# A two-layer graph attention kernel: the order of one superchunk's work within a step

## The chip, the cores and the metric

The kernel runs on one core of one Trainium2 chip. The metric is the device time of one execution in microseconds. The times before are the median of three runs; one more execution was taken with the profiler. In the text PE is TensorE, DVE is VectorE, ACT is ScalarE, POOL is GpSimd and SP is SyncE, the queue that issues most of the plain DMAs.

## The reference

A graph network of two attention layers over 6250 nodes with 256 features, and 200,000 edges that are sorted by destination. For each layer:

```
te  = relu(edge_attr @ We + be) * exp(x @ Wo + bo)[src]
hx  = x @ Wg                                    # 4 heads of 64, then 1 head of 256
al  = leaky_relu((hx . a_s)[src] + (hx . a_d)[dst] + (te @ Wge) . a_e, 0.2)
m   = segment_max(al, dst)
al  = exp(al - m[dst]);  al = al / segment_sum(al, dst)[dst]
out = segment_sum(hx[src] * al, dst) + b
```

Each node has a self loop as well, whose edge term is the mean of its incoming ones. Layer 0 gives relu(out + x), layer 1 adds its input, and residuals of x go on top. A layer norm with a relu stands at the front.

## The kernel before, in words

**Tiles.** The edges of a layer are cut into chunks of 128 and 24 chunks make a superchunk (C = 24); 66 superchunks make a layer. The loop in `edges` goes over the superchunks of both layers, one *step* for each. In a step `st` is the superchunk that is summed, `nx` the one behind it, `pv` the one ahead. The function `ending` writes the last three superchunks of each layer by hand.

**What a superchunk goes through.** `gather` (24 indirect DMAs on POOL, line 1065) brings the source rows of each edge into G; there are three G buffers, so a gather waits until the sums that read its buffer have ended. `spread` (DVE, lines 1189 and 1190) makes one-hot blocks lb and Q from the destinations, for two superchunks at a time. `parts` (line 1304) splits the destinations' logits into three bf16 parts on DVE and multiplies them by Q on PE. `blocks` (DVE, line 1311) lays the result out as aq. `rphase1` (lines 1165 and 1166) makes relu(edge_attr @ We) as y on PE and R on ACT, in two halves; `rphase2` (line 1174) adds its share of the edge logits into the PSUM tile zad, and `adst` (line 1318) the destinations' share, as lb times aq. `edge_rows` (lines 1332 and 1335) transposes zad into rt on DVE, and `logits` (lines 1346 to 1363) makes the logits al and their running maxima fb. `ends` (PE, line 1370) transposes these into the tile lf; `links` (lines 1380 to 1387) runs them over the chunk's rows by two scans on DVE and transposes back; `maxima` (lines 1397 to 1423) takes the maxima and exponentials. `scale` (layer 0, DVE, line 1454) multiplies G by the weights, all 24 chunks in one instruction of 128 x 6144; `scale_rows` (layer 1, ACT, line 1463) does it chunk by chunk. `carried` (lines 1436 to 1444) adds what the superchunk ahead has left for a node that both share. `sums` (PE, line 1473) multiplies the 24 one-hots S, which `onehots` made (DVE, line 1283), by G into u, one matmul of two passes for a chunk. `evict` (ACT, line 1478) copies u to U. `finish` (DVE and ACT, lines 1489 to 1640, transposes at line 1563) does the nodes of `pv`.

**What sets the order.** Each engine takes its instructions in the order in which the code issues them; the framework adds the semaphore waits. So the order of calls in the loop of `edges` is the order on every engine. Before the change a step issues: gather(nx), logits(st), ends(st), spread(nx), parts(nx), the first half of rphase1(nx), links(st), rows2, loads, blocks(nx), maxima(st), the second half of rphase1, rphase2(nx), adst(nx), scale or scale_rows(st), carried(st), sums(st), rows3, onehots(nx), finish(pv), evict(st), edge_rows(nx). The tile lf is one PSUM bank: `ends` writes its columns 1 to 128, and `links` its columns from 160 on.

Of the kernel before, what the change touches and what calls it, by code (L numbers as in the profile page):

```python
# [22 lines left out]
F32 = mybir.dt.float32  # L23
# [8 lines left out]
P = 128  # L32
C = 24
# [48 lines left out]
class Kernel:  # L82
# [705 lines left out]
    def edges(self, ctx):  # L788
        nc = self.nc
        steps = self.steps  # L790
        if self.NS % 2:
            self.load_lb(1)
        pv = late = None
        self.ahead, self.rest = 1, None
        for k, st in enumerate(steps):
            nx = steps[k + 1] if k + 1 < len(steps) else None
            if st["s"] + 2 >= self.NS:
                continue
            for q in steps[k + 1:k + 3]:
                if q["L"] is st["L"] and "tw" not in q:  # L800
                    self.nodes(q)
            self.load_lb(k + 2)
            left = 99
            if self.ahead < len(self.groups):
                left = self.groups[self.ahead][0] - 2 - (self.ahead + 2 >= len(self.groups)) - k
            if self.rest is None and left <= 2:
                gi = self.index_load(self.ahead, self.xp)
                self.rest = self.index_group(self.ahead, self.xp, gi)
            if st["L"].l and (st["s"] == 2 or st["s"] + 3 == self.NS) and not hasattr(self, "flag_i"):
                self.flag()  # L810
                if self.early:
                    self.window()
            if st["s"] + 3 == self.NS:
                self.ending(st, *steps[k + 1:k + 3], pv, late, steps[k + 3] if k + 3 < len(steps) else None)
                pv = late = None
                continue
            if 3 <= k + 1 < 6 and nx["L"].l == 0:
                nx["own"] = steps[k - 2]["G"]
            if k:
                self.gather(nx)  # L820
                st["rows"] = st["L"].l
                drain(self.logits(st))
                self.ends(st)
            self.spread(nx)
            self.parts(nx)
            y = self.rphase1(nx)
            next(y)
            if k:
                self.links(st)
            if late:  # L830
                self.rows2(late)
            self.load_fl(k + 1)
            self.blocks(nx)
            if k:
                drain(self.maxima(st))
            drain(y)
            self.load_ea(k + 2)
            self.rphase2(nx)
            self.adst(nx)
            if "S" not in st:  # L840
                self.onehots(st)
            if k:
                if st["rows"]:
                    self.scale_rows(st)
                else:
                    drain(self.scale(st))
                self.carried(st)
                self.sums(st)
            if late:
                self.rows3(late)  # L850
                late = None
            self.onehots(nx)
            if pv:
                drain(self.finish(pv))
            self.evict(st)
            if pv:
                self.rows1(pv)
                late = pv
            self.index_on(left)
            if k == 4 and self.early:  # L860
                self.lacking()
            if k >= 6:
                next(self.late, None)
                next(self.late, None)
            self.edge_rows(nx)
            if st["s"] + 4 == self.NS:
                drain(self.finish(st))
            pv = st
# [279 lines left out]
    def rphase1(self, st):  # L1148
# [11 lines left out]
        for a, b in self.pieces(c):  # L1160
# [5 lines left out]
            nc.scalar.activation(R[:, :, w], y[:, :, :n], AF.Relu, bias=self.be[l])  # L1166
            yield

    def rphase2(self, st):

        nc, l, R = self.nc, st["L"].l, st["R"]
        for w, o in self.halves(st):
            for i in range(2):
                nc.tensor.matmul(st["zad"][i * PH:(i + 1) * PH, o], self.wea[l][0], R[:, i, w],  # L1174
                                 start=True, stop=False)
# [107 lines left out]
            nc.vector.tensor_tensor(st["S"][:, c0:c1, :], self.k_iota.unsqueeze(1).to_broadcast(w),  # L1283
                                    self.loc[:, o + c0:o + c1].unsqueeze(2).to_broadcast(w), op=OP.is_equal)

    def parts(self, st):

        L, V = st["L"], self.nc.vector
        H = L.H
        if "a3" not in st:  # L1290
            q = [q for q in self.steps[st["k"]:st["k"] + 2 - st["k"] % 2] if q["L"] is L and "tw" in q]
            n, i = len(q), st["k"] % 4
            ad = self.tw4[:, i:i + n, L.ad:L.ad + H]
            a3 = self.wp.tile([P, 2, 4, 3], BF, name="a3")
            r = self.wp.tile([P, 2, 4], F32, name="a3r")
            V.tensor_copy(a3[:, :n, :H, 0], ad)
            V.tensor_sub(r[:, :n, :H], ad, a3[:, :n, :H, 0])
            V.tensor_copy(a3[:, :n, :H, 1], r[:, :n, :H])
            V.tensor_sub(a3[:, :n, :H, 2], r[:, :n, :H], a3[:, :n, :H, 1])
            for j, t in enumerate(q):  # L1300
                t["a3"] = a3[:, j]
        a3 = st["a3"]
        st["zad"] = z = self.ps_1.tile([P, 1024], F32, name="zad")
        self.nc.tensor.matmul(z[:, 400:400 + 3 * H], st["Q"], a3[:, :H, :].rearrange("p h t -> p (h t)"),  # L1304
                              start=True, stop=True)

    def blocks(self, st):

        H = st["L"].H
        st["aq"] = aq = self.aq[st["k"] % 2]  # L1310
        self.nc.vector.tensor_tensor(aq[:, :, 4:4 + 3 * H],
                                     st["zad"][:, 400:400 + 3 * H].unsqueeze(1).to_broadcast([P, 4, 3 * H]),
                                     self.quad.unsqueeze(2).to_broadcast([P, 4, 3 * H]), op=OP.mult)

    def adst(self, st):
# [149 lines left out]
    def sums(self, st, *parts):  # L1465
        nc, L, c = self.nc, st["L"], st["C"]
        G, S = st["G"], st["S"]
        for a, b in parts or ((0, c),):
            for i in range(a, b):
                j = st["n"] = st.get("n", -1) + 1  # L1470
                if j == 0 and "u" not in st:
                    st["u"] = self.ps_1.tile([P, 512], F32, name="u")
                nc.tensor.matmul(st["u"][:, :L.W], S[:, i, :], G[:, i, 0:L.W], start=(j == 0), stop=(j == c - 1))  # L1473
# [282 lines left out]
def drain(g):  # L1756
    for _ in g:
        pass
# [85 lines left out]
```

## Time and profile before

| | before |
|---|---|
| median of 3 runs | 4928.91 us (4916.35 to 4935.57) |
| profiled execution | 4925.46 us |
| its span | 4923.7 us |
| granted TensorE clock | 0.725 of full speed |
| PE busy | 2940.4 us, 60% |
| DVE busy | 2462.7 us, 50% |
| ACT busy | 1132.2 us, 23% |
| POOL busy | 2989.0 us, 61% |
| DMA, mean over the span | 120 GB/s |

The span is the time between the first and the last instruction of the profiled execution. A row of a timeline gives the start, the duration, the engine and line, the operation, the tile written and the tiles read, with shapes, and in brackets how long the engine was idle before and what ended that. "issue" means that the engine waited for nothing that the profile shows, and "remote" a releaser that is not resolved. A row of the waits gives the engine, the tile and line that waited, what it waited for, the microseconds in total, how many times, and the longest. Layer 0's even steps run from about 335 to 2374 us, layer 1's from about 2699 to 4838 us.

### The profile page before, as it was taken

To read this page: it belongs to the slowest core of one execution; us is meant where nothing else is said; L and a number is where in the kernel's file an instruction comes from. 1 tells how busy PE (TensorE), PEld (TensorE's weight loads), DVE (VectorE), ACT (ScalarE), POOL (GpSimd) and SP (SyncE) were. 2 spreads that over 40 slices of the span, in tenths; PEclk is the share of its full clock that TensorE was granted. 3 is DMA by queue.
4 is the path that set the end of the run, shared out by engine and by line. 5 is a ranking of instruction groups with operands and counts; after the bars stand their busy time and mean duration, and the time that the engine had idled before them with its cause. 6 is when DMAs were issued, how large, how long until landed. Compare 5 with 4: busy or idle time off the path is not lost.

```text
span 4923.7 us, 38114 instructions
## 1 busy us (share of the span) xinstructions
PE 2940.4 (60%) x10100; PEld 1841.8 (37%) x10100; DVE 2462.7 (50%) x6148; ACT 1132.2 (23%) x2701; POOL 2989.0 (61%) x3216
## 2 busy tenths in 40 slices
PE   6655666666666666665646556555565555655656
PEld 5433433343333434343434333333333333333334
DVE  5556666676666666666734323333333332333335
ACT  4211111111111111111103323233233332323322
POOL 6356666666666666666544656656666666666663
PEclk8777777777777777777777667667667676666767
DMA  7144444444444444444433434434444443443442
GB/s 223 55 119 125 126 128 134 123 135 132 133 124 128 135 126 131 129 135 122 122 109 92 121 106 115 122 105 119 114 118 114 112 121 107 116 118 107 118 117 71
DMA packets 248253, 591.97 MB, mean 120 GB/s; under 512 B 65849, under 2 KB 105125, under 8 KB 247783
## 3 DMA queue, kind: packets, MB, share of 16 engines
q0 software_dynamic: 150048, 422.51, 32.7%
q1 hardware_dynamic: 97009, 164.82, 10.5%
q10 hardware_dynamic: 976, 2.12, 0.2%
q8 instruction: 86, 1.41, 0.1%
q14 instruction: 134, 1.10, 0.1%
HBM read 544.23 MB, written 45.36 MB: 120 GB/s over the span
## 4 chain that ended last, share of the span: by engine, by line
issue 29%; PE 28%; DVE 21%; POOL 13%; another core or an unknown queue 5%; DMA 3%; ACT 1%; SPq 0%; DVEq 0%; ACTq 0%; POOLq 0%
PE u L1473 21%; POOL G L1065 12%; DVE G L1454 7%; DMA G<-T,src 3%; PE y L1165 2%; DVE S L1283 2%; PE zad L1174 2%; DVE m L1402 1%; DVE lb L1189 1%; DVE rt L1332 1%; ACT R L1166 1%; DVE t1rows L1638 1%; DVE fb L1397 0%; PE lf L1370 0%
## 5 line engine op out<-in xcount | busy, mean ns | idle before, releaser
L1065 POOL DMA_INDIRECT G<-T,src x3066 | 2912.9, 950 | 1824.8 <-issue 949.2
L1473 PE MATMUL u<-G,S 128*128 128x270 f32 (+1 forms) x6212 | 1873.3, 448 | 1419.9 <-issue 1202.2
L1473 PEld LDWEIGHTS u<-G,S 128*128 128x128 f32 x6212 | 1355.8, 221 | 1871.8 <-issue 1438.5
L1463 ACT ACTIVATE G<-G,kw 128x256 f32<-128x256 f32 x1512 | 609.0, 496 | 0.0
L1380 DVE TENSOR_TENSOR_SCAN cl<-fl,cl,lf 4x129 f32<-4x129 f32 (+1 forms) x130 | 61.1, 470 | 1007.6 <-PE zad L1304 940.1
L1478 ACT ACTIVATE U<-u 128x270 f32<-128x270 f32 (+1 forms) x130 | 51.0, 393 | 2169.3 <-PE u L1473 1686.5
L1454 DVE TENSOR_TENSOR G<-G,kps 128x6144 f32<-128x6144 f32 (+6 forms) x86 | 441.7, 5150 | 0.0
L1283 DVE TENSOR_TENSOR S<-kps,loc 128x3072 f32<-128x3072 f32 (+1 forms) x135 | 438.1, 3245 | 4.7
L1165 PE MATMUL y<-ea,webd 64*128 64x256 f32 (+2 forms) x1056 | 355.0, 762 | 41.0 <-ACT R L1166 35.3
L1174 PE MATMUL zad<-R,wea 128*64 128x384 f32 (+1 forms) x1056 | 285.0, 677 | 156.6 <-issue 87.5
L1166 ACT ACTIVATE R<-y,webd 128x1024 f32<-128x1024 f32 (+3 forms) x264 | 235.4, 892 | 427.5 <-PE y L1165 161.9
L1174 PEld LDWEIGHTS zad<-R,wea 128*64 128x64 f32 x1056 | 82.9, 177 | 395.8 <-issue 263.4
L1505 DVE SCALAR_TENSOR_TENSOR mg<-U,mw 128x1 f32<-128x1 f32 x65 | 14.4, 221 | 364.1 <-remote 170.6
L1165 PEld LDWEIGHTS y<-ea,webd 64*128 64x128 f32 x1056 | 116.0, 269 | 105.6 <-issue 59.3
L1332 DVE STREAM_TRANSPOSE rt<-zad 128x768 f32<-128x768 f32 (+1 forms) x130 | 125.8, 968 | 5.4 <-remote 5.4
L567 PE MATMUL fin<-wg,h1T 128*128 128x260 f32 x264 | 116.8, 587 | 1.5 <-ACT h1T L1565 1.5
L1189 DVE TENSOR_TENSOR lb<-lb,kps 128x1536 bf16<-128x1536 bf16 (+1 forms) x68 | 112.9, 1661 | 0.0
L1436 DVE SCALAR_TENSOR_TENSOR G<-U,kw,G 1x257 f32<-1x257 f32 x62 | 29.5, 476 | 152.4 <-issue 87.0
L1575 ACT ACTIVATE t1rows<-t1rows 128x1 f32<-128x1 f32 x66 | 13.4, 203 | 363.9 <-DVE t1rows L571 147.4
L1370 PE MATMUL lf<-ident,fb 128*36 128x128 f32 (+1 forms) x132 | 52.0, 394 | 55.8 <-DVE fb L1363 45.6
L1318 PE MATMUL zad<-lb,aq 128*128 128x384 bf16 (+2 forms) x264 | 83.8, 409 | 0.0
L1515 ACT ACTIVATE mw<-mw 128x8 f32<-128x8 f32 x66 | 13.8, 209 | 298.7 <-issue 146.9
(275 smaller groups left out, 2366.7 us busy)
## 6 DMA issues: line engine op xcount, KB each, us to landing
ea<-in_ea_dram SPq DMA_DIRECT2D x64, 768.0 KB
G<-T,src POOLq DMA_INDIRECT x3066
lb<-locrow SPq DMA_DIRECT2D x64, 384.0 KB
nd<-t1rows SPq DMA_DIRECT2D x66, 225.8 KB
tw<-nd SPq DMA_DIRECT2D x66, 225.8 KB
tw<-T SPq DMA_DIRECT2D x66, 117.2 KB
T<-t1rows SPq DMA_DIRECT2D x66, 113.8 KB
tw<-in_x_dram SPq DMA_DIRECT2D x66, 112.0 KB
```

The lines of the kernel that those rows point to most:

```text
L567: self.nc.tensor.matmul(ps[:, :L.MW], hT[:, k, :], self.wg[L.l][:, k, :], start=(k == 0), stop=(k == 1))
L1065: nc.gpsimd.indirect_dma_start(out=G[:, c, 0:L.TW], out_offset=None, in_=st.get("from", self.T[L.l])[0:self.N, :], in_offset=bass.Indirect ...
L1165: nc.tensor.matmul(y[:, i, :n], self.webd[l][r, :], ea[r, w], start=True, stop=True)
L1166: nc.scalar.activation(R[:, :, w], y[:, :, :n], AF.Relu, bias=self.be[l])
L1174: nc.tensor.matmul(st["zad"][i * PH:(i + 1) * PH, o], self.wea[l][0], R[:, i, w], start=True, stop=False)
L1189: V.tensor_tensor(lb[:, :, :n], lb[:, :, :n], self.k_part.unsqueeze(2).to_broadcast([P, i, n]), op=OP.is_equal)
L1283: nc.vector.tensor_tensor(st["S"][:, c0:c1, :], self.k_iota.unsqueeze(1).to_broadcast(w), self.loc[:, o + c0:o + c1].unsqueeze(2).to_broad ...
L1318: self.nc.tensor.matmul(st["zad"][:, o], st["aq"].rearrange("p k j -> p (k j)"), st["lb"][:, w], start=False, stop=True)
L1332: V.transpose(rv[:, :32 * c].rearrange("p (b n) -> p b n", b=2), z.rearrange("p (b n) -> p b n", b=2)[:, :, :16 * c])
L1454: nc.vector.tensor_tensor(v, v, pw[:, c0:c1, :].unsqueeze(3) .to_broadcast([P, c1 - c0, H, L.F]), op=OP.mult)
L1463: self.nc.scalar.activation(v, v, AF.Copy, scale=st["w"][:, c:c + 1])
L1473: nc.tensor.matmul(st["u"][:, :L.W], S[:, i, :], G[:, i, 0:L.W], start=(j == 0), stop=(j == c - 1))
```

## The change

In a step, links, the first half of rphase1 and maxima now come first. In layer 0 the scaling is cut into two halves of 12 chunks with `carried` between them; `spread` comes behind, then the sums of 14 chunks, `parts` and `blocks`, the sums of 5 chunks, `adst`, and the sums of the last 5. In layer 1 `scale_rows` goes ahead of the second half of rphase1; the sums of 8 chunks come, then `spread` and `parts`, the other 16 chunks, and behind them `rphase2`, `onehots`, `blocks` and `adst`. The product of `parts` lies in columns 240 on of the bank lf, and zad is taken when it is first needed. The first step of all keeps its order.

```diff
-            self.spread(nx)
-            self.parts(nx)
+            else:
+                self.spread(nx)
+                self.parts(nx)
             y = self.rphase1(nx)
             next(y)
             if k:
@@
             self.load_fl(k + 1)
-            self.blocks(nx)
             if k:
                 drain(self.maxima(st))
-            drain(y)
-            self.load_ea(k + 2)
-            self.rphase2(nx)
-            self.adst(nx)
+            else:
+                self.blocks(nx)
+            if k and st["rows"]:
+                self.scale_rows(st)
+                drain(y)
+                self.load_ea(k + 2)
+            else:
+                drain(y)
+                self.load_ea(k + 2)
+                self.rphase2(nx)
             if "S" not in st:
                 self.onehots(st)
-            if k:
-                if st["rows"]:
-                    self.scale_rows(st)
-                else:
-                    drain(self.scale(st))
+            if not k:
+                self.adst(nx)
+                self.onehots(nx)
+            elif st["rows"]:
                 self.carried(st)
-                self.sums(st)
+                self.sums(st, (0, C // 3))
+                self.spread(nx)
+                self.parts(nx, self.lf)
+                self.sums(st, (C // 3, C))
+                self.rphase2(nx)
+                self.onehots(nx)
+                self.blocks(nx)
+                self.adst(nx)
+            else:
+                f = self.scale(st, cuts=(0, C // 2, C))
+                next(f)
+                self.carried(st)
+                drain(f)
+                self.spread(nx)
+                self.sums(st, (0, 14))
+                self.parts(nx, self.lf)
+                self.blocks(nx)
+                self.sums(st, (14, 19))
+                self.adst(nx)
+                self.sums(st, (19, C))
+                if late:
+                    self.rows3(late)
+                    late = None
+                self.onehots(nx)
             if late:
                 self.rows3(late)
                 late = None
-            self.onehots(nx)
...
-    def parts(self, st):
+    def parts(self, st, bank=None):
...
-        st["zad"] = z = self.ps_1.tile([P, 1024], F32, name="zad")
-        self.nc.tensor.matmul(z[:, 400:400 + 3 * H], st["Q"], a3[:, :H, :].rearrange("p h t -> p (h t)"),
+        if bank is None:
+            self.zad(st)
+        st["ad"] = z = st["zad"][:, 400:400 + 3 * H] if bank is None else bank[:, 240:240 + 3 * H]
+        self.nc.tensor.matmul(z, st["Q"], a3[:, :H, :].rearrange("p h t -> p (h t)"),
                               start=True, stop=True)
```

PE in a step of layer 0, before, from the sums of one superchunk to those of the next. The LDWEIGHTS of Q and the matmul of a are `parts`, the matmuls of fin and wg are `finish` and the next layer's node rows, zad from R is `rphase2` and zad from aq is `adst`:

```order
L1473 MATMUL u<-G,S 128x270 x24
L1563 MATMUL fin<-ident,fb 128x128 x2
L1370 MATMUL lf<-ident,fb_195 36x128
L1304 LDWEIGHTS Q
L1304 MATMUL zad<-a_6577,Q 128x12
L1165 MATMUL y<-ea,webd_119 128x256 x2
L1387 MATMUL lf<-ident,cl_189 128x36
L567 MATMUL fin<-wg_894,h1T 128x260 x2
L1165 MATMUL y<-ea,webd_119 128x512 x2
L1174 MATMUL zad<-R,wea_142 64x384 x4
L1318 LDWEIGHTS aq_199
L1318 MATMUL zad<-lb,aq_199 128x384
```

The same engine and layer after the change, from `links` to the last sums:

```order
L1422 MATMUL lf<-ident,cl_190 128x36
L567 MATMUL fin<-wg_894,h1T 128x260 x2
L1192 MATMUL y<-ea,webd_119 128x512 x2
L1207 MATMUL zad<-R,wea_142 64x384 x4
L1508 MATMUL u<-G,S 128x270 x14
L1339 LDWEIGHTS Q
L1339 MATMUL lf<-a_6656,Q 128x12
L1508 MATMUL u<-G,S 128x270 x5
L1353 LDWEIGHTS aq_198
L1353 MATMUL zad<-lb,aq_198 128x384
L1353 LDWEIGHTS aq_198
L1353 MATMUL zad<-lb,aq_198 128x384
```

`parts` and `adst` have moved from ahead of the sums to behind their 14th and their 19th chunk; five chunks follow.

DVE in a step of layer 0, after the change, from the second half of the scaling on; aq from lf is `blocks`, and "waits PE" is a wait for PE's semaphore:

```order
L1489 TENSOR_TENSOR G<-G,kps 128x12x256
L1222 TENSOR_TENSOR lb<-lb,kps 128x1536 [waits DMAHW0_49]
L1223 TENSOR_TENSOR Q<-kps,qsel 128x256
L1329 CAST a_3667<-tw_203 128x8 [waits DMAHW7_49]
L1330 TENSOR_TENSOR a3r<-tw_203,a_3667 128x8 [waits DVE_49]
L1331 CAST a_3667<-a3r 128x8 [waits DVE_49]
L1332 TENSOR_TENSOR a_3667<-a3r,a_3667 128x8 [waits DVE_49]
L1346 TENSOR_TENSOR aq_198<-lf,quad 128x4x12 [waits PE_49]
L571 TENSOR_TENSOR t1rows<-fin,bias_898 128x260 [waits DMAHW5_49,DMAHW4_49]
L1313 COPY kps<-lastloc 128x1
L1316 TENSOR_TENSOR S<-kps,loc 128x3072 [waits DVE_49]
L1524 TENSOR_SCALAR cnt<-U 128x1
```

`blocks` stood between links and maxima and now stands behind the scaling, with rows3, onehots, finish, the transpose rt and the logits queued behind it.

PE in a step of layer 1, after the change:

```order
L1508 MATMUL u<-G,S 128x261 x8
L1339 LDWEIGHTS Q
L1339 MATMUL lf<-a_15150,Q 128x3
L1508 MATMUL u<-G,S 128x261 x16
L1207 MATMUL zad<-R,wea_145 64x384 x4
L1353 LDWEIGHTS aq_199
L1353 MATMUL zad<-lb,aq_199 128x384
L1353 LDWEIGHTS aq_199
L1353 MATMUL zad<-lb,aq_199 128x384
L1405 MATMUL lf<-ident,fb_195 33x128
L1192 MATMUL y<-ea,webd_900 128x256 x2
L1422 MATMUL lf<-ident,cl_190 128x33
```

Here `rphase2` and `adst`, which stood ahead of the sums, follow them, and lf, from which links starts, comes behind.

More of the change, by code (lines that the diff above doesn't have):

```diff
@@ L1167, in rphase1, with zad @@
             yield
+    def zad(self, st):
+        if "zad" not in st:
+            st["zad"] = self.ps_1.tile([P, 1024], F32, name="zad")
     def rphase2(self, st):
+        self.zad(st)
         nc, l, R = self.nc, st["L"].l, st["R"]
@@ L1302, in parts @@
         a3 = st["a3"]
-        st["zad"] = z = self.ps_1.tile([P, 1024], F32, name="zad")
-        self.nc.tensor.matmul(z[:, 400:400 + 3 * H], st["Q"], a3[:, :H, :].rearrange("p h t -> p (h t)"),
+        if bank is None:
+            self.zad(st)
+        st["ad"] = z = st["zad"][:, 400:400 + 3 * H] if bank is None else bank[:, 240:240 + 3 * H]
+        self.nc.tensor.matmul(z, st["Q"], a3[:, :H, :].rearrange("p h t -> p (h t)"),
                               start=True, stop=True)
@@ L1311, in blocks @@
         self.nc.vector.tensor_tensor(aq[:, :, 4:4 + 3 * H],
-                                     st["zad"][:, 400:400 + 3 * H].unsqueeze(1).to_broadcast([P, 4, 3 * H]),
+                                     st["ad"].unsqueeze(1).to_broadcast([P, 4, 3 * H]),
                                      self.quad.unsqueeze(2).to_broadcast([P, 4, 3 * H]), op=OP.mult)
```

## The prediction

> **What bounds the kernel now.** First the page's groups and its chain, then the waits of both layers' steady steps, then the timeline of single steps.
>
> ```profile
> L1065 POOL DMA_INDIRECT G<-T,src x3066 | 2912.9, 950 | 1824.8 <-issue 949.2
> issue 29%; PE 28%; DVE 21%; POOL 13%; another core or an unknown queue 5%; DMA 3%; ACT 1%; SPq 0%; DVEq 0%; ACTq 0%; POOLq 0%
> ```
>
> No engine is busy throughout, and the largest share of the chain is "issue", time without a visible cause. The gathers take 0.95 us each and idle 0.30 us between them ("issue"), so 24 of them take 24 × 1.25 = 30 us per step. The waits of layer 0 (335 to 2374 us, first two rows) and of layer 1 (2699 to 4838 us):
>
> ```profile
> POOL G L1065 <- PE fin L1563: 217.1, 35, 25.0
> POOL G L1065 <- PE u L1473: 138.4, 22, 9.2
> POOL G L1065 <- PE zad L1304: 376.5, 58, 8.3
> ```
>
> Once per step POOL waits for PE, on average 6 us: the G buffer is free when the sums before last have ended. So a step is 30 us of gathers and a wait for the end of the sums. Its length comes from the evictions:
>
> ```profile
> 334.89 0.40 ACT L1478 ACTIVATE U<-u 128x270 f32<-128x270 f32 x1 [3.11 <-PE u L1473]
> 2373.84 0.40 ACT L1478 ACTIVATE U<-u 128x270 f32<-128x270 f32 x1 [12.10 <-PE u L1473]
> 2698.95 0.39 ACT L1478 ACTIVATE U<-u 128x261 f32<-128x261 f32 x1 [20.02 <-PE u L1473]
> 4838.28 0.39 ACT L1478 ACTIVATE U<-u 128x261 f32<-128x261 f32 x1 [21.38 <-PE u L1473]
> ```
>
> Layer 0: 2038.95 us over 58 steps, 35.15 each. Layer 1: 2139.33 over 59, 36.26 each. Why the sums end so late, a layer 0 step shows:
>
> ```profile
> 1018.79 0.94 POOL L1065 DMA_INDIRECT G<-T,src  x1 [4.69 <-PE fin L1563]
> 1022.72 6.54 DVE L1454 TENSOR_TENSOR G<-G,kps 128x6144 f32<-128x6144 f32 x1
> 1026.20 0.50 PE L1318 MATMUL zad<-lb,aq 128*128 128x384 bf16 x2
> 1030.03 0.20 DVE L1444 SCALAR_TENSOR_TENSOR G<-U,slink,G 1x5 f32<-1x5 f32 x1
> 1030.29 13.44 PE L1473 MATMUL u<-G,S 128*128 128x270 f32 x45 [3.60 <-DVE crow L1442]
> 1030.68 3.36 DVE L1283 TENSOR_TENSOR S<-kps,loc 128x3072 f32<-128x3072 f32 x1
> 1041.23 0.97 DVE L1332 STREAM_TRANSPOSE rt<-zad 128x768 f32<-128x768 f32 x1
> 1047.72 0.94 POOL L1065 DMA_INDIRECT G<-T,src  x1 [0.30 <-issue]
> 1049.46 0.61 PE L1473 MATMUL u<-G,S 128*128 128x270 f32 x1 [2.47 <-issue]
> 1053.57 0.94 POOL L1065 DMA_INDIRECT G<-T,src  x1 [4.90 <-PE fin L1563]
> ```
>
> The 45 passes (two per chunk) take 13.44 us, 0.30 each, and then the last ones come one by one with 2.5 us of "issue" between. PE is stuck until some 5 us after the last gather at 1047.72; POOL goes on 34.8 us after its restart. Layer 1 is alike:
>
> ```profile
> 3607.05 0.47 DVE L1380 TENSOR_TENSOR_SCAN cl<-fl,cl,lf 1x129 f32<-1x129 f32 x1 [16.01 <-PE zad L1304]
> 3607.07 0.94 POOL L1065 DMA_INDIRECT G<-T,src  x1 [7.00 <-PE zad L1304]
> 3612.15 9.67 ACT L1463 ACTIVATE G<-G,kw 128x256 f32<-128x256 f32 x24
> 3612.31 2.83 PE L1174 MATMUL zad<-R,wea 128*64 128x384 f32 x8 [1.21 <-issue]
> 3615.07 0.82 PE L1318 MATMUL zad<-lb,aq 128*128 128x384 bf16 x2
> 3615.68 8.60 PE L1473 MATMUL u<-G,S 128*128 128x261 f32 x36
> 3626.49 0.98 DVE L1332 STREAM_TRANSPOSE rt<-zad 128x768 f32<-128x768 f32 x1
> 3628.34 0.59 PE L1473 MATMUL u<-G,S 128*128 128x261 f32 x1 [3.12 <-issue]
> 3641.07 2.77 PE L1473 MATMUL u<-G,S 128*128 128x261 f32 x6 [1.53 <-issue]
> 3644.12 0.94 POOL L1065 DMA_INDIRECT G<-T,src  x1 [7.25 <-PE zad L1304]
> 3649.66 0.60 PE L1473 MATMUL u<-G,S 128*128 128x261 f32 x2
> 3679.13 0.94 POOL L1065 DMA_INDIRECT G<-T,src  x1 [5.21 <-PE zad L1304]
> ```
>
> Here 36 passes run freely, those from 3624 crawl, and at 3641.07, 34.0 us after the restart, PE is free. One more place shows that what crawls is also PE's signals to other engines. POOL gathered without a long pause up to 309:
>
> ```profile
> 290.31 0.27 PE L1370 MATMUL lf<-ident,fb 128*36 128x128 f32 x1
> 308.98 0.40 ACT L1478 ACTIVATE U<-u 128x270 f32<-128x270 f32 x1 [23.47 <-issue]
> 309.22 0.94 POOL L1065 DMA_INDIRECT G<-T,src  x1 [0.59 <-issue]
> 312.52 0.47 DVE L1380 TENSOR_TENSOR_SCAN cl<-fl,cl,lf 4x129 f32<-4x129 f32 x1 [20.45 <-remote]
> 323.64 11.21 PE L1473 MATMUL u<-G,S 128*128 128x270 f32 x48 [1.01 <-DVE G L1444]
> ```
>
> The sums that stand ahead of lf were through at 290.3, but ACT evicted them only at 308.98, and DVE took lf at 312.52, 22 us late. With POOL silent (the wait of 25.0 among the waits, up to 335) all 48 passes of 323.64 run without a pause and the eviction follows at once (334.89). So I read: while gathers run, PE's signals back up, PE itself goes on until something is full (36 passes in layer 1, 17 us after the restart; 45 in layer 0), and what it finished is heard by the others only 34 us after the restart. The backing up must begin before PE is stuck, so before +17.
>
> **The change, part by part.**
>
> *Layer 0, the order on PE.* Before, parts and blocks of the next superchunk stand at the step's start and adst ahead of the sums: all is heard early. After, PE does 14 chunks, the matmul of parts, 5 chunks, adst, 5 chunks; adst waits for blocks on DVE, and blocks for parts on PE. This is a new round trip PE to DVE to PE in the midst of the gathers. Scale in halves lets the sums start 3.3 us sooner (half of 6.54), so +8.2 after POOL's restart instead of +11.5; 28 passes at 0.30 end at +16.6, and parts' signal stands in line behind what they left. I take it that it is heard, and blocks starts, at +34.0. From there the path is: blocks and hand-overs 0.3; adst 0.50 to 0.82; the last 10 passes 3.0 (at 0.30) to 4.6 (at 2.77/6); and what is left of chunks 14 to 19 when PE is stuck, 0 to 2.7 (38 passes are needed; 45 ran freely here, 36 in layer 1; at most I allow six at 0.46, as in 3641.07). The sum is 37.8 to 42.4 us. I take 39.5, near the low end, since the freely running 45 passes are layer 0's own row: 4.35 over 35.15, and 58 × 4.35 = +252 us (ends 58 × 2.65 = +154 and 58 × 7.25 = +420).
>
> Behind blocks on DVE stand onehots, finish, rt and the logits, which now run after +34 instead of under the sums. From onehots (1030.68) to the end of rt (1042.20) is 11.5 us, so lf comes no earlier than 34.2 + 11.5 = 45.7, which is 6.2 in the next gathers. Links to sums were 11.5 and are 8.2: the sums start at 14.4, their 14th chunk ends at 22.8, still ahead of 34.0. So this costs nothing more as long as it stays within those 11 us; the upper end holds the case that it doesn't.
>
> Spread's group on the page, with 68 instructions for 132 superchunks:
>
> ```profile
> L1189 DVE TENSOR_TENSOR lb<-lb,kps 128x1536 bf16<-128x1536 bf16 (+1 forms) x68 | 112.9, 1661 | 0.0
> ```
>
> *Spread, parts' casts, rows3 and carried between the halves* lie on DVE beside the first 14 chunks (8.4 us of PE). Were DVE later than PE there, PE would wait ahead of +34, which costs nothing as long as it waits to +34 anyway; without that wait it is at most spread's 1.66 us in every second step. POOL's and SP's issues keep their order but for the load of ea, a few rows up. Nothing for these.
>
> *Layer 1.* Parts goes behind 8 chunks, but blocks stands behind the sums, so PE doesn't wait in their midst. What costs is that rphase2 and adst, ahead of the sums before, now follow them, and rt, the logits, lf and links wait for them. Behind the sums' end: rphase2 up to 2.83, adst 0.82, rt 0.98, then the logits. Before, rt stood in the shadow of the sums (3626.49) and links began with POOL's restart (3607.05 against 3607.07). So links come 4.6 us later by these rows, and by the logits on top, but rphase2 and adst (3.65) no longer stand between links and sums, and ACT's scaling no longer waits behind the second R. The sums start 0 to 3 us later. Of a later start the two steps shown give the price: started 8.61 after the restart, the step took 37.05; started 5.54 after it, 35.01: 0.66 per us. That is 0 to +2.0 us; I add 0.5 to the upper end for the two instructions of parts that now stand within the sums. I take +1.3, past the middle since the logits' own time isn't in the 4.6: 59 × 1.3 = +77 (0 to +148).
>
> The sum: 4925.46 + 252 + 77 = 5254. The profiled execution lies 3.45 under the median 4928.91 (span 4923.7, the rest about the ends), so 5258 against the median; I say 5255. Ends of this case: 4929 + 154 = 5083 to 4929 + 568 = 5497.
>
> A clock row speaks for a gain in layer 0:
>
> ```profile
> 1030.00:1036.00 6.00, 5.71 (x13) 4.36 (x14) 5.50 (x16) 0.81 (x3) 4.73 (x5) 0.50 0.67 178
> ```
>
> After 3.60 us without a matmul the granted clock is 0.50 and 13 passes take 5.71 us, 0.44 each, against 11.21/48 = 0.23 for the quiet row. If PE idles less before the sums, these 13 cost 2.7 us less. The Trainium skill ("TensorE: Matmul & The Clock Gate", section "Why this matters for your kernels") warns of idle gaps over about 3 us between bursts; the row agrees, and by that rule the halves would spare 2.7 us of each step's sums. Those 2.7 us end before the stuck stretch and are worth something only in the first rival.
>
> **The rivals.**
>
> 1. *The round trip is heard in time (faster).* Parts' matmul at +16.6 is at the edge of the stretch; if DVE hears it at once, PE doesn't wait, and the earlier, warmer sums (3.3 + 2.7 us) all end before +34.0. Then every layer 0 step is POOL's 34.0 and 0.5 for the hand-over: 58 × (34.5 − 35.15) = −38, and layer 1 from 0 to a gain of −0.5 per step if the scaling's earlier start wins, half of that taken (59 × 0.25 = 15): 4929 − 38 − 15 = 4876. It decides if PE's signals at +17 take under 5 us. Against it: 290.31 to 312.52. For it: at the step's start DVE follows PE at once (3607.05 beside 3607.07). The Trainium skill ("Advanced Engine Details and Errata", section "Network/Comms") puts the reading of a semaphore at 50 to 100 ns; by that rule the round trip would be free and this rival the forecast, but the 22 us of the row disagree. Chance 0.15.
> 2. *It cancels.* As 1, but layer 1 pays 0.6: 4929 − 38 + 35 = 4926. Chance 0.05.
> 3. *Late, but not to the end.* PE's signals trickle, blocks hears after 10 us, at +27, and chunks 19 to 24 crawl to +36.5: 58 × 1.35 + 59 × 0.6 = +114, so 5043. Chance 0.14.
>
> **How the numbers follow.** The forecast (blocks waits to +34, layer 1 links late) has 0.66. Range 4900 to 5480: it takes in 2, 3 and the forecast's ends but its last 17 us, and leaves out rival 1 (0.15) and some 0.04 above. The likeliest case's own range is 5083 to 5497. This kernel's measurements tell 0.5% (25 us) from no change. Faster by over that 0.15, within it 0.05, slower 0.14 + 0.66 = 0.80.
>
> **What would show it.** Right: in layer 0, PE idle of over 10 us before adst (L1353), released by DVE aq; DVE idle as long before blocks (L1346); evictions 38 to 42 us apart; in layer 1, rt right behind adst and links 5 us or more after POOL's restart. Wrong: blocks within 2 us of parts' matmul, sums without a wait at chunk 19, layer 0 evictions 34.5 us apart.

## The result and the profile after

| | before | after |
|---|---|---|
| median | 4927.24 us (4 runs, 4916.35 to 4935.57) | 5173.3 us (4 runs, 5165.34 to 5179.9) |
| profiled execution | 4925.46 us | 5174.47 us |
| its span | 4923.7 us | 5172.7 us |
| granted TensorE clock | 0.725 | 0.724 |

The change makes the kernel slower: the ratio is 1.05, 95% interval 1.0474 to 1.0526. The page after, the rows for the gathers, the chain and `blocks` (in group rows: busy time and mean ns, then the engine's idle time ahead of them and what ended most of it):

```profile
PE 23%; DVE 23%; issue 20%; another core or an unknown queue 17%; POOL 12%; DMA 3%; ACT 2%; DVEq 0%; SPq 0%; ACTq 0%; POOLq 0%
L1092 POOL DMA_INDIRECT G<-T,src x3066 | 2916.6, 951 | 2063.0 <-PE u L1508 1014.9
L1346 DVE TENSOR_TENSOR aq<-lf,quad 128x12 bf16<-128x12 f32 (+1 forms) x125 | 24.0, 192 | 1996.1 <-remote 1532.7
```

The gathers take as long as before (0.951 us each), but POOL idles 2063.0 us between them instead of 1824.8, 238 us more. `blocks`, which had no row of its own on the page before, now has DVE idle for 1996.1 us ahead of it. The same four evictions as before (the 4th, 61st, 68th and 127th of the run) in the timeline after:

```profile
340.38 0.38 ACT L1513 ACTIVATE U<-u 128x270 f32<-128x270 f32 x1
2615.49 0.38 ACT L1513 ACTIVATE U<-u 128x270 f32<-128x270 f32 x1
2947.29 0.39 ACT L1513 ACTIVATE U<-u 128x261 f32<-128x261 f32 x1 [1.66 <-PE u L1508]
5084.40 0.39 ACT L1513 ACTIVATE U<-u 128x261 f32<-128x261 f32 x1 [1.61 <-PE u L1508]
```

Layer 0's steps went from 2039 to 2275 us, layer 1's from 2139 to 2137, the start from 335 to 340, the passage between the layers from 325 to 332, the end from 85 to 88. Of 249 us between the profiled executions layer 0's 57 even steps hold 236: 35.77 us each before, 39.91 after. Layer 1's 59 steps are 36.26 and 36.22. Mean steps below are taken between the same evictions.

The waits of layer 0's steps after, columns as in the prediction:

```profile
ACT t1rows L1610 <- DVE t1rows L571: 1175.2, 57, 23.1
DVE aq L1346 <- remote: 797.7, 57, 16.6
POOL G L1092 <- PE u L1508: 567.1, 57, 11.8
```

In each of 57 steps of layer 0 DVE waits for `blocks`' input, 14.0 us on average, ACT waits for what is queued behind `blocks` (t1rows), and POOL waits 9.9 us for the sums instead of some 6. One step of layer 0 after, from POOL's restart at 1016.12 (below, +34 means 34 us after such a restart):

```profile
1016.12 0.94 POOL L1092 DMA_INDIRECT G<-T,src  x1 [9.81 <-PE u L1508]
1024.88 0.47 DVE L1415 TENSOR_TENSOR_SCAN cl<-fl,cl,lf 4x129 f32<-4x129 f32 x1 [0.49 <-PE lf L1405]
1028.11 1.64 PE L1192 MATMUL y<-ea,webd 64*128 64x512 f32 x4
1029.81 1.11 ACT L1193 ACTIVATE R<-y,webd 128x1024 f32<-128x1024 f32 x1 [1.59 <-PE y L1192]
1032.80 6.65 PE L1508 MATMUL u<-G,S 128*128 128x270 f32 x28 [0.31 <-issue]
1039.29 0.17 PE L1339 MATMUL lf<-a,Q 128*128 128x12 bf16 x1
1041.68 0.19 PEld L1508 LDWEIGHTS u<-G,S 128*128 128x128 f32 x1 [1.94 <-issue]
1043.08 0.61 PE L1508 MATMUL u<-G,S 128*128 128x270 f32 x1 [2.42 <-issue]
1044.49 0.29 PEld L1508 LDWEIGHTS u<-G,S 128*128 128x128 f32 x1 [2.62 <-issue]
1050.08 1.96 PE L1508 MATMUL u<-G,S 128*128 128x270 f32 x4 [0.79 <-issue]
1050.61 0.21 DVE L1346 TENSOR_TENSOR aq<-lf,quad 128x48 bf16<-128x48 f32 x1 [11.75 <-remote]
1051.83 0.85 PE L1353 MATMUL zad<-lb,aq 128*128 128x384 bf16 x2
1052.47 2.75 PE L1508 MATMUL u<-G,S 128*128 128x270 f32 x10
1055.49 0.94 POOL L1092 DMA_INDIRECT G<-T,src  x1 [9.33 <-PE u L1508]
```

The matmul of `parts` is through at 1039.46, and DVE takes its result at 1050.61, 11.15 us later and 34.49 after POOL's restart. Behind it stand adst, the last ten passes and POOL's release, 4.88 us; the step takes 39.37. ACT had still taken y 0.06 us after its end, at 1029.81, 13.7 after the restart. PE meanwhile hangs: from 1040 to 1050 its weight loads and passes come 1.40 us apart (1041.68, 1043.08, 1044.49).

### The profile page after: what moved, and what is told of

Same layout as the page of the kernel before. It is cut to its first block, busy times and chain, and to the rows that moved or that the text cites. A ratio compares the mean times of both kernels' runs of the same rounds, so it can differ in the third digit from the quotient of the medians.

```text
span 5172.7 us, 38155 instructions
## 1 busy us (share of the span) xinstructions
PE 3079.2 (60%) x10100; PEld 1871.9 (36%) x10100; DVE 2473.1 (48%) x6210; ACT 1136.0 (22%) x2701; POOL 2991.4 (58%) x3216
## 4 chain that ended last, share of the span: by engine, by line
PE 23%; DVE 23%; issue 20%; another core or an unknown queue 17%; POOL 12%; DMA 3%; ACT 2%; DVEq 0%; SPq 0%; ACTq 0%; POOLq 0%
PE u L1508 16%; POOL G L1092 12%; DVE G L1489 6%; DVE S L1316 3%; PE y L1192 3%; DMA G<-T,src 3%; PE zad L1207 1%; DVE rt L1367 1%; PE ps L567 1%; DVE m L1437 1%; DVE lb L1222 1%; ACT G L1498 1%; PE lf L1405 1%; PE fin L567 1%
## 5 line engine op out<-in xcount | busy, mean ns | idle before, releaser
L1092 POOL DMA_INDIRECT G<-T,src x3066 | 2916.6, 951 | 2063.0 <-PE u L1508 1014.9
L1508 PE MATMUL u<-G,S 128*128 128x270 f32 (+1 forms) x6212 | 1935.4, 457 | 1053.1 <-issue 905.8
L1346 DVE TENSOR_TENSOR aq<-lf,quad 128x12 bf16<-128x12 f32 (+1 forms) x125 | 24.0, 192 | 1996.1 <-remote 1532.7
L1489 DVE TENSOR_TENSOR G<-G,kps 128x3072 f32<-128x3072 f32 (+7 forms) x148 | 450.1, 3049 | 0.0
L1192 PE MATMUL y<-ea,webd 64*128 64x256 f32 (+2 forms) x1056 | 396.1, 845 | 40.6 <-issue 26.3
L1538 ACT ACTIVATE mw<-mw,mg 128x2 f32<-128x2 f32 x66 | 19.6, 298 | 951.0 <-DVE mg L1537 885.0
L1405 PEld LDWEIGHTS lf<-ident,fb 128*36 128x36 f32 (+1 forms) x132 | 15.1, 114 | 530.7 <-DVE fb L1398 385.6
L1598 PE MATMUL fin<-ident,fb 128*128 128x128 f32 x132 | 34.9, 354 | 197.7 <-ACT fb L1587 173.7
L567 PE MATMUL fin<-wg,h1T 128*128 128x260 f32 x264 | 134.5, 663 | 1.5 <-ACT h1T L1600 1.5
```

What stands on the lines that cost most here:

```text
L567: self.nc.tensor.matmul(ps[:, :L.MW], hT[:, k, :], self.wg[L.l][:, k, :], start=(k == 0), stop=(k == 1))
L1092: nc.gpsimd.indirect_dma_start(out=G[:, c, 0:L.TW], out_offset=None, in_=st.get("from", self.T[L.l])[0:self.N, :], in_offset=bass.Indirect ...
L1192: nc.tensor.matmul(y[:, i, :n], self.webd[l][r, :], ea[r, w], start=True, stop=True)
L1405: self.nc.tensor.transpose(self.lf[0:e.shape[1], 1:P + 1], e, self.ident)
L1489: nc.vector.tensor_tensor(v, v, pw[:, c0:c1, :].unsqueeze(3) .to_broadcast([P, c1 - c0, H, L.F]), op=OP.mult)
```

## The experiments

**Each layer's part, and two smaller steps of layer 0, on one chip.** In e1_l1_only layer 0 keeps the order of before, in e2_l0_only layer 1 does. e4_halves takes of the change only layer 0's scaling in halves:

```diff
-                    drain(self.scale(st))
-                self.carried(st)
+                    f = self.scale(st, cuts=(0, C // 2, C))
+                    next(f)
+                    self.carried(st)
+                    drain(f)
```

e3_parts_early has, on top of that, adst in layer 0 between the sums; `parts` and `blocks` stay at the step's start:

```diff
-            self.adst(nx)
...
-                self.sums(st)
+                self.sums(st, (0, 19))
+                self.adst(nx)
+                self.sums(st, (19, C))
```

> Layer 0 in the order of before, layer 1 in the order of the change. Round-trip theory (all of the loss is layer 0's blocks, heard 34 us after POOL's restart): layer 1's steps stay at 36.2 us as in the changed kernel, so 4915 to 4945 us. Rival (the loss is spread over both layers, layer 1's being hidden in the changed kernel by something layer 0 left): over 4960.

> Layer 0 in the order of the change, layer 1 in the order of before. Round-trip theory: 5160 to 5190 us, layer 0's evictions 39.9 us apart, layer 1's 36.2. Rival: under 5130.

> Layer 1 as before. Layer 0 keeps the halves of the scaling, carried between them and adst behind the 19th chunk, but spread, parts and blocks stand at the step's start as before, so that PE needs no answer of DVE within the sums. Round-trip theory: blocks no longer waits; sums start some 3 us sooner than before; layer 0's steps 34.5 to 35.7, 4855 to 4930 us. Rival (what costs is the sums cut by adst, or the halves): over 5000 us.

> The order of before, and only layer 0's scaling in halves with carried between them; adst ahead of the sums. Round-trip theory with POOL's floor of 34.5 per step: only the steps with late logits gain, 0 to 1.3 us per step, 4855 to 4930 us. Rival (sums start sooner, PE stays warm, and each step gains the 3 us): 4760 us.

What came tells nothing about the parts of the change, and more than I had asked about the chip. On this chip the kernel before took 4016.92 us (31 runs), not 4927, and none of the four differed: 4013.88 (ratio 0.9992, 0.9982 to 1.0001), 4019.8 (1.0006, 0.9997 to 1.0016), 4014.51 (0.9993, 0.9984 to 1.0003) and 4014.59 us (0.9997, 0.9988 to 1.0007). A step takes 29.7 us in layer 0 and 29.8 to 30.0 in layer 1 in all of them. The page of e2_l0_only, chain and gathers, and a step of its layer 0, which has the change's order:

```profile
POOL 42%; issue 17%; PE 14%; DVE 13%; ACT 10%; DMA 5%; DVEq 0%; ACTq 0%; POOLq 0%; SPq 0%
L1104 POOL DMA_INDIRECT G<-T,src x3066 | 2919.9, 952 | 971.8 <-issue 914.4
...
1012.84 6.65 PE L1520 MATMUL u<-G,S 128*128 128x270 f32 x28
1019.33 0.17 PE L1351 MATMUL lf<-a,Q 128*128 128x12 bf16 x1
1019.36 2.52 PE L1520 MATMUL u<-G,S 128*128 128x270 f32 x10
1019.54 0.21 DVE L1358 TENSOR_TENSOR aq<-lf,quad 128x48 bf16<-128x48 f32 x1 [3.49 <-PE lf L1351]
```

Here `blocks` starts 0.04 us after the end of parts' matmul. No pass crawls: PE idles 25.6 us in all ahead of the 6212 passes of the run, against 1053.1 in the changed kernel above. POOL idles little more than its 0.30 us between gathers (971.8 us for 3066 of them), so the gathers set the length of the steps, and none of these orders of the other engines counted. There are thus two kinds of measurement: where PE's signals are heard in time (before near 4017 us) and where they are late (before near 4927). Below, a chip is called late or in time by what it showed when it was measured. The split of the loss by layers rests on the changed kernel's own trace, 57 steps of layer 0 and 59 of layer 1; e1_l1_only and e2_l0_only were measured in time only.

**The same on a second chip.** e5_early_again is the kernel of e3_parts_early. In e6_parts_first, layer 1 is as before, and in layer 0 the change's spreading, parts and blocks come ahead of all sums:

```diff
-                drain(f)
                 self.spread(nx)
-                self.sums(st, (0, 14))
                 self.parts(nx, self.lf)
+                drain(f)
                 self.blocks(nx)
-                self.sums(st, (14, 19))
+                self.sums(st, (0, 19))
```

> The kernel with spread, parts and blocks at the step's start and layer 0's scaling in halves, run again, since the first four kernels met a state of the chip in which PE's signals are not late at all (before 4017 us, not 4927). If signals are late here as in the first measurement (before near 4927): round-trip theory 4850 to 4935 us, the rival that the cut sums or the halves cost over 5000. If they are not late (before near 4017): 4015 again, and nothing is told apart.

> Layer 1 as before; layer 0 as in the change, but spread, parts' matmul and blocks go between the halves of the scaling and ahead of all sums, so that parts' signal has no sums' passes ahead of it; adst stays behind the 19th chunk. With late signals (before near 4927): if the signals queue behind what PE has done, blocks hears parts within 5 us and layer 0's steps are 34.5 to 36, 4855 to 4950; if every signal after some 10 us of gathers is late to +34, blocks waits as in the change and it is 5120 us or more. With signals in time (before near 4017): 4010 to 4040.

Signals in time again: before 4022.79 us, the two 4018.55 (0.999, 0.9978 to 1.0001) and 4023.01 (0.9997, 0.9986 to 1.0008), steps 29.7 and 30.0. It separates nothing, but it is a second chip of the kind that is in time. On each chip all executions were of one kind. No chip of the experiments was measured at two times, so that the kind belongs to the chip isn't shown.

**With fewer gathers.** In h_before and h_after one plain DMA of table rows replaces 11 of the 24 gathers of each steady superchunk (so these rows of G aren't the sources' own); h_before has the order of before, h_after that of the change:

```diff
+            cs = [c for c in cs if not 0 < c < 12]
+            nc.gpsimd.dma_start(out=G[:, 1:12, 0:L.TW],
+                                in_=self.T[L.l][0:11 * P, :].rearrange("(c p) w -> p c w", p=P))
```

> The order of before, with 11 of the 24 indirect gathers of most superchunks taken away (chunks 1 to 11 get rows 0 to 1407 of the table by one plain DMA instead of the rows of their edges; the rest of the work is the same). POOL then needs some 18 us per step. If PE's signals are in time, the engines' own chain is the bound, 25 to 26 us in layer 0 and 21 to 22 in layer 1: 3050 to 3250 us. If signals are late while POOL gathers, they are late only to some +22: 3100 to 3400 us.

> The order of the change with the same gathers taken away. Round-trip theory: with signals in time the order costs nothing even where the engines are the bound, within 1% of the other (steps of 25 to 26.5 and 21 to 22 us); with late signals blocks waits to some +22, chunks 19 to 24 follow, and it is 2 to 5 us per layer 0 step slower, 110 to 290 us. Rival (the new order makes the engines' chain itself longer by what stands behind blocks on DVE): over 3% slower than the other even with signals in time.

This chip was of the late kind (before: 4939.4 us). h_before took 3491.85 us and h_after 3676.76, 185 us or 5.3% more. Steps of layer 0: 25.83 and 28.40; layer 1: 21.71 and 22.14. A step of h_after, and `blocks` in the last of its 57 steps of layer 0, which still has all 24 gathers:

```profile
1029.61 0.95 POOL L1097 DMA_INDIRECT G<-T,src  x1 [0.30 <-issue]
1034.69 0.17 PE L1344 MATMUL lf<-a,Q 128*128 128x12 bf16 x1
1034.89 0.21 DVE L1351 TENSOR_TENSOR aq<-lf,quad 128x48 bf16<-128x48 f32 x1 [3.49 <-PE lf L1344]
...
1947.43 0.21 DVE L1351 TENSOR_TENSOR aq<-lf,quad 128x48 bf16<-128x48 f32 x1 [14.63 <-remote]
```

The last gather of the step starts at 1029.61, parts' matmul at 1034.69, and DVE hears it 0.03 us after its end: on a late chip too, once POOL is silent. In all 56 steps with 13 gathers it is 0.04 to 0.07 us. In the last step, with 24, parts' matmul ends at 1936.25, while POOL still gathers, and DVE hears it at 1947.43, 11.18 us later and at +34.38; POOL goes on at +38.94, as in the full kernel. So the same order in the same run has the late signal with 24 gathers and doesn't have it with 13. And a second cost shows. Without that last step layer 0 takes 25.67 us per step in h_before and 28.20 in h_after: with no late signal in the way the new order is 2.53 us longer, because links waits for rt, the logits and what stands behind `blocks`. In the full kernel this chain of 28.20 us lies under the 30 us of gathers, which fits that it shows nowhere on the chips with signals in time.

**Two orders between before and after, on a late chip.** e3_parts_early_late_signals is the kernel of e3_parts_early. e8_blocks_behind has layer 1 as before, and in layer 0 the change's order but for blocks and adst, which go behind all sums and the eviction:

```diff
                 self.parts(nx, self.lf)
-                self.blocks(nx)
-                self.sums(st, (14, 19))
-                self.adst(nx)
-                self.sums(st, (19, C))
+                self.sums(st, (14, C))
...
+            if k and not st["rows"]:
+                self.blocks(nx)
+                self.adst(nx)
             self.edge_rows(nx)
```

> Layer 1 as before; layer 0 with the halves, carried between them and adst behind the 19th chunk, but spread, parts and blocks at the step's start. If signals are late here (before near 4930): round-trip theory 4850 to 4935 us, layer 0's steps 34.5 to 35.7; the rival that the cut sums or the halves cost: over 5000 us. If they are not late (before near 4017): 4015 again.

> Layer 1 as before; layer 0 as in the change with parts behind the 14th chunk, but blocks and adst behind finish, ahead of rt: PE has no answer of DVE to wait for within the sums, and DVE does onehots and finish before it waits for parts. Round-trip theory with late signals: the sums end near +34.5 as before, POOL goes on then, but rt, the logits and lf follow blocks and adst by 5 us, so the next sums start at some +13.5: 34.5 to 37 per layer 0 step, 4855 to 5000 us, well under the change's 5173. The rival that parts inside the sums is enough to cost the 4 us per step: over 5120 us. With signals in time: 4010 to 4040.

Before took 4909.28 us here, e3's order 4989.98 (ratio 1.017, 1.0153 to 1.0187) and e8's 5024.59 (1.0245, 1.022 to 1.027). Both lie outside what I had expected: e3's just under the "over 5000" of its rival (the cut sums or the halves cost), e8's above its 5000. Against before on this chip the two orders cost 81 and 115 us. Layer 0's mean steps are 37.07 and 37.34 (layer 1's 35.96 and 36.06). A step with e3's order and the beginning of the next:

```profile
1009.72 0.94 POOL L1110 DMA_INDIRECT G<-T,src  x1 [11.03 <-PE fin L1616]
1017.66 8.93 PE L1526 MATMUL u<-G,S 128*128 128x270 f32 x38 [1.79 <-DVE crow L1495]
1026.42 0.49 PE L1371 MATMUL zad<-lb,aq 128*128 128x384 bf16 x2
1026.75 2.21 PE L1526 MATMUL u<-G,S 128*128 128x270 f32 x9
1029.56 0.39 PE L1526 MATMUL u<-G,S 128*128 128x270 f32 x1 [0.60 <-issue]
1043.74 0.98 DVE L1385 STREAM_TRANSPOSE rt<-zad 128x768 f32<-128x768 f32 x1 [12.27 <-remote]
1043.85 0.40 ACT L1531 ACTIVATE U<-u 128x270 f32<-128x270 f32 x1 [13.85 <-remote]
1044.08 0.94 POOL L1110 DMA_INDIRECT G<-T,src  x1 [4.29 <-remote]
1050.20 0.47 DVE L1433 TENSOR_TENSOR_SCAN cl<-fl,cl,lf 4x129 f32<-4x129 f32 x1
1058.77 6.42 PE L1526 MATMUL u<-G,S 128*128 128x270 f32 x27
```

This is the plainest picture of a late signal: all 48 passes are through at 1029.95, 20.2 us after POOL's restart, and ACT, DVE and POOL go on at 1043.74 to 1044.08, 34 us after it. PE was done 13.8 us before any engine heard. So sums that end early are worth nothing here, and rt, whose input was ready at 1026.9, comes at +34.0. The next step pays: links at +6.1, sums from +14.7. The steps alternate (34.4 here, up to 41.0 in others). With e8's order, `blocks` waits like that of the change, but nobody in the midst of the sums waits for it:

```profile
1034.41 0.17 PE L1351 MATMUL lf<-a,Q 128*128 128x12 bf16 x1
1047.64 0.21 DVE L1358 TENSOR_TENSOR aq<-lf,quad 128x48 bf16<-128x48 f32 x1 [7.37 <-remote]
1049.01 0.95 POOL L1104 DMA_INDIRECT G<-T,src  x1 [5.01 <-PE u L1520]
```

POOL restarts at 1014.03 and 1049.01, 34.98 apart. Against it the change, with adst and ten passes behind `blocks`, is 39.91 − 37.34 = 2.57 us per step longer, 146 us in 57 steps. The two were measured on different chips, whose before differ by 18 us, which is 0.3 us per step of layer 0. (That it is nearly the number of h_before and h_after again is chance: there no signal is late.) e8's own 1.57 over the 35.77 of before is open. The late rt alone doesn't explain it: links is at +4.4 on average against +1.3, but the sums start at +12.8 against +12.6; what differs more is that some 36 passes run freely where 42 did. No run takes it by itself.

**Two runs that would have closed the list.** e9_halves_again is the kernel of e4_halves (it halves the scaling; the maxima stay whole), e10_parts_first_again that of e6_parts_first.

> The halves alone: layer 0's maxima and fb scaling in halves, so that its sums start earlier, with parts, blocks and adst where the kernel before has them, ahead of the sums. My theory (what the change moves behind or between the sums hears PE only some 34 us after POOL's restart, on a chip where PE's signals come late): nothing that PE must send inside a step is waited for anew, so layer 0's mean step is 34.4 to 35.8 against 35.77, layer 1's is that of before, and the time is 0 to 80 us under that of before (4850 to 4930 for a before of 4930). Rival (sums that start earlier are themselves the harm, since PE then sends more of its signals while POOL gathers): layer 0's step is over 36.5 and the time at least 40 us over before. On a chip where before takes some 4020, both: within 5 us of before.

> Layer 1 as in the kernel before. In layer 0 the change's spreading, parts and blocks are put ahead of all the step's sums instead of between passes 28 and 29 (adst stays where the change has it, ahead of the last 5 chunks). Where PE's signals come late: theory A (PE's signals queue behind one another, so that only what lies behind many passes is late) says that the parts' signal is heard some 10 us after they run, adst is done by +25, and layer 0's mean step is 36.5 to 37.5 (time 4960 to 5010 for a before of 4930). Theory B (whatever PE sends later than about +10 us is heard only some 34 us after POOL's restart, however few instructions are ahead of it) says that blocks still come at +34 and the step is 38.5 to 40 (5080 to 5170). On a chip where before takes some 4020, both: within 10 us of before.

The chip was one with signals in time (before 4016.78 us): 4015.86 (1.0001, 0.9991 to 1.001) and 4017.03 us (1.0002, 0.9992 to 1.0012). Both are the common expectation for such a chip and decide nothing. So it stays open whether the halves alone help or harm where signals are late, and whether parts put ahead of the sums would be heard early. On theory B as it is worded the trace of the changed kernel has something to say; it stands in the last section.

## Why the prediction was right, and where it was off

**The round trip** was right, and its step too. `blocks` was put at +34.0 and came at +34.33 on average, between +34.02 and +34.73 in every one of the 57 steps. From there to POOL's restart I had summed 3.8 to 8.4 us and taken 5.5; the step shown has 4.88 (hand-over 1.22, adst 0.64, ten passes 2.75, the rest 0.27). The step was forecast at 39.5 and is 39.91. That the lateness is the cause and not the order alone, two controls show: layer 0's same order costs nothing where `blocks` hears PE within 0.04 us (e2_l0_only, where the gathers set the step), and on a late chip `blocks` hears PE in 0.03 us with 11 of the 24 gathers gone and 11.18 us late in the one step that keeps them (h_after). The forecast was 5255 us and 5173.3 was measured, 82 less: layer 1 was put 79 too high and layer 0 16, and 15 us outside the steps were left out; the other 2 lie between medians and profiled executions.

**A slip in counting.** Between the evictions at 334.89 and 2373.84 lie 57 steps, not the 58 I divided by, so before's layer 0 step was 35.77 and not 35.15. With it the forecast's own term is 57 × (39.5 − 35.77) = +213 and not +252; measured are +236. The nearness of 252 to 236 is thus partly luck. Rival 1's layer 0 term would have been 57 × (34.5 − 35.77) = −72 instead of −38, and its total some 4842.

**Layer 1** is the term that was mis-sized: +77 forecast, −2 measured. The mechanism came: rt right behind adst, links 5.6 us after POOL's restart:

```profile
3635.53 0.94 POOL L1092 DMA_INDIRECT G<-T,src  x1 [7.15 <-PE u L1508]
3637.49 0.50 PE L1353 MATMUL zad<-lb,aq 128*128 128x384 bf16 x2
3638.03 0.98 DVE L1367 STREAM_TRANSPOSE rt<-zad 128x768 f32<-128x768 f32 x1 [2.40 <-PE zad L1353]
3641.16 0.47 DVE L1415 TENSOR_TENSOR_SCAN cl<-fl,cl,lf 1x129 f32<-1x129 f32 x1 [0.51 <-issue]
3645.14 4.80 PE L1508 MATMUL u<-G,S 128*128 128x261 f32 x16
3649.80 5.09 PE L1508 MATMUL u<-G,S 128*128 128x261 f32 x22
3669.46 2.09 PE L1508 MATMUL u<-G,S 128*128 128x261 f32 x4 [0.81 <-issue]
3669.51 0.18 DVE L1346 TENSOR_TENSOR aq<-lf,quad 128x12 bf16<-128x12 f32 x1 [21.20 <-PE u L1508]
```

The sums start 9.6 us after the restart (9.56 on average of 59 steps, 7.76 before). What failed is the price, 0.66 us per us of a later start, read off two steps of before. Within before it holds roughly: a straight line through its 59 steps of layer 1 gives 0.53. It doesn't hold from the one order to the other. Before's sums start between +5.4 and +8.6 and PE has its first pause of over 0.45 us between +13.9 and +17.8, but always after 36 to 39 passes. So in this layer PE gets stuck after so many instructions more than after so much time. (In layer 0 of before the number varies, 31 to 46.) After the change 38 passes run freely in the step shown, where 36 did in the step of before (39.0 and 37.2 on average), as rphase2 and adst no longer use up that number ahead of them; PE gets stuck at +20.0 on average instead of +16.4, and four passes are left at +33.9 instead of six. The later start and the longer run cancel. `blocks` waits to +34 here too, but behind the sums, where nobody in the step needs it. That the cancelling comes from the count is argued from these rows; no run changed it alone.

**The halves.** The clock came as reckoned. The sums' first 28 passes after, a window with the granted clock third from the end of the row:

```profile
1032.80:1039.40 6.60, 6.60 (x30) 5.43 (x30) 5.96 (x7) 0.00 (x0) 5.08 (x6) 1.00 0.41 110
```

The clock is 1.00 where the row of before had 0.50, and 28 passes take 6.65 us, 0.24 each; 13 passes thus save 13 × (0.44 − 0.24) = 2.6 us. It was worth nothing in these steps, as said, since `blocks` comes at +34 all the same. The rule of the Trainium skill that was weighed there ("TensorE: Matmul & The Clock Gate", section "Why this matters for your kernels") was right about the passes and silent on the step.

**DVE's queue.** Links was forecast at +6.2 and is at +7.8 on average, the sums at +14.4 and are at +16.4; both still ahead of +34, so this cost nothing more, as said. h_after shows the price where it isn't covered, 2.53 us per step.

**The signs.** DVE idle over 10 us before `blocks` and evictions 38.7 to 41.4 us apart came. PE idle over 10 us before adst did not: adst follows the burst at 1051.83, and PE spent the time crawling through chunks 14 to 19, which I had priced only as what is left of them at +34.

**The rivals.** The first was written for signals in time; it is right that DVE follows at once there, but its gain didn't come there either, since the gathers bound each step. The Trainium skill's 50 to 100 ns for reading a semaphore ("Advanced Engine Details and Errata", section "Network/Comms") are near the 0.04 us of e2_l0_only and far from the 11.15 us here. The third (late, but not to the end) has no row for it: `blocks` came no earlier than +34.02 in any step of layer 0. Start, passage and end, +15 us together, I had not priced.

## What to carry to other kernels

In this kernel a round trip between two engines in the midst of the gathers cost what the slowest signal of that stretch cost, not what its instructions did: look in the trace for a result that is done and taken up late before putting one there. What another engine must answer cost less ahead of that stretch (81 us over before in e3's order) or behind it (115 in e8's) than in its midst (246 in the change), and none of the three was faster than before where signals are late. Here a wait to the same moment cost some 2.6 us per step more with adst and ten passes behind it (the change against e8's order), and nothing in layer 1, where that work isn't needed within the step. A time on one chip alone can mislead: the change costs 5% where signals are late, and layer 0's part of it nothing where they are in time. A mean step is divided by a count of steps taken from the trace.

## What the chip showed that I had not expected

The same kernel takes 4017 to 4023 us on three chips and 4909 to 4939 on two others and where it was first timed, with gathers of 0.95 us each on both. The rows for the gathers' DMA queue, of the changed kernel (late) and of e2_l0_only (in time):

```profile
q0 software_dynamic: 150048, 422.51, 31.0%
q0 software_dynamic: 150048, 422.51, 40.5%
```

The packets' time is the same, 31.0% of 5172.7 us (1604) and 40.5% of 4025.2 (1630), so the time in the packets isn't what differs. On the late chips PE's results are heard soon after they are done early in a step's gathers: in the changed kernel PE ends the second half of y at +10.6 to +15.0, and ACT takes it within 0.1 us in 47 of the 57 steps of layer 0 and 0.3 to 2.5 us late in ten, at +17.3 at the latest. That speaks against theory B as worded, by which whatever PE sends after about +10 us is heard at +34, however little is ahead of it. What PE finishes at +17.2 behind 38 passes (adst of e3's order, 1026.9) is heard only at +34, some 4 us after the last gather, and PE's own instructions come 1.40 us apart once it is stuck.

Nor is it PE's signals alone. Two rows of DVE from the step of before that the prediction shows; the second takes al from the first:

```profile
1048.51 0.33 DVE L1350 TENSOR_TENSOR al<-al,ade 128x96 f32<-128x96 f32 x1 [1.08 <-DVE al L1348]
1050.19 0.26 DVE L1352 SCALAR_TENSOR_TENSOR al<-al 128x96 f32<-128x96 f32 x1 [1.35 <-DVE al L1350]
```

DVE waits 1.35 us for its own result. So it does, 1.07 to 1.35 us, in each of the 25 steps of before's layer 0 in which that result is done between +25 and +31; in the other 31 that the trace has, and in all of e2_l0_only and h_before, it is 0.03 to 0.04 us. DVE's signals at +25 to +31 are thus a microsecond late where PE's wait to +34. That PE's stand in line behind those of its many passes would fit this, but no run shows it. What sets a chip's kind is open too: no run here changes it.
